# Macaron block on one core: where the output products, the query products, the value tiles and GpSimd's order stand

## The chip, the core and the metric

The kernel runs on one core of a Trainium2 chip. The core has five engines that run their own instruction streams: TensorE (PE; its weight loads are shown as PEld), VectorE (DVE), ScalarE (ACT), GpSimd (POOL) and SyncE (SP), which here only issues transfers. The metric is the device time of one execution in microseconds (us), median of several runs. Lower is better.

## The reference, cut to what matters

All data are float32. A block with half-weighted feed-forward parts on both sides of an attention:

```python
x = x + 0.5 * ffn(layernorm(x))          # x: 4 batches x 256 tokens x 512
x = x + attn(layernorm(x))
x = x + 0.5 * ffn(layernorm(x))

def attn(x):                             # 32 query heads, 8 key/value heads, head size 128
    q, k, v = x @ wq, x @ wk, x @ wv     # wq: 512 x 4096, wk and wv: 512 x 1024
    q, k = rope(q), rope(k)
    scores = einsum('bqhgd,bshd->bhgqs', q by groups of 4 heads, k) * 128 ** -0.5
    allowed = (j <= i) & (j > i - 128)   # causal, a window of 128 keys
    out = einsum('bhgqs,bshd->bqhgd', softmax(where(allowed, scores, min)), v)
    return out @ wo                      # wo: 4096 x 512

def ffn(x):                              # base 512 x 512 with bias, 8 low-rank experts of rank 16
    w = top-2 of softmax(x @ W_router.T), renormalised
    return x @ W_base.T + b_base + 2.0 * sum over experts of w * ((x @ A_e.T) @ B_e.T)
```

## The kernel before, in words

The 1024 tokens are eight tiles of 128. They are worked on in two halves `h` of two batches each. Around the attention stands the feed-forward part (`ffn`), cut into one-letter steps (M, X, T, N: normalise and transpose; A: low-rank products; R: the routing, many small VectorE instructions; B: base product; G, L: the gated part and the sum). The strings in `loose` place the second feed-forward part's steps in the last units of the attention loop.

The attention loop runs over *units* `u`, that is `(h, g, b)`: half, key/value group (8 of them, 4 query heads each), batch of the half. A group's two units have `b` = 0 and 1. In the loop `n` is the number of the *next* group, counted from 1. So `n` is odd in one group and even in the other, and a unit with `b = 0` holds the query products of group `n`. A unit with `b = 1` and even `n` holds the key products of two groups.

Three matrix products are done with seven half-size products in place of eight (a Strassen form), for which sums of blocks are made first:

- `queries`: product `n` of seven, 8 matmul instructions each. `product(1)` is copied by ScalarE (`p1c`), `product(6)` added to it (`u2`), and so on. The four results stand in four PSUM banks of the tag `mm`, one for each batch and pair of heads. `turn(b, j, bank)` calls `rope`: three VectorE instructions (`ra`, L368, and two `rb`, L370) that read the bank, and one GpSimd addition (L374) into `qT`.
- `keys`: the same for two groups of keys, in two banks.
- `outputs`: four entries for one unit, `(4)`, `(1, 6)`, `(2, 3)` and `(7, 5)`, named y4, y(1,6), y(2,3), y(7,5) in this text. y4 is 4 matmul instructions, the others 8 each. Each takes one `mm` bank, and VectorE then adds it to `x` (L624) or `z` (L617). They use sums of `oT` (`oTs`, four GpSimd instructions, L120) and sums of `wo` (`wos`, four GpSimd instructions, L125, in `sum_o_weights`). Product 4 reads the fourth of the `wos` instructions' result, product 6 the third `oTs`, product 7 the first `wos`. The entries are put in the queue `late` at the end of a unit, and run in the next one.

Further parts of a unit: `project_v` (pv, L492: a value tile for a later group), `scores` (sa L509 and sb L524 on TensorE; L515 to L531 on VectorE), `exponentials` (`nm`, L537 and L538 on VectorE; L542 on ScalarE), `normalize` (two GpSimd instructions, L551), `transposes` (t, L560; then a ScalarE copy `p0` and two VectorE products L569), and `values` (oa and ob, L582, and two ScalarE copies into `oT`). `scores` of the next unit stand between the `transposes` and the `values` of this one.

What sets the order: inside `tc.manual_schedule(engines=...)` the named engines issue in program order. Elsewhere the framework's list scheduler orders each engine by its own estimate of times: among the instructions that it holds for ready, the one that stands first in the program goes first, and another one may fill a wait. In the kernel before, GpSimd and ScalarE are in program order from the loop on (L732). TensorE and VectorE are left to the list scheduler, and so is GpSimd in the projections ahead of the loop (L696 to L708). Tiles of one tag are handed out in program order. There are four banks of the tag `mm` and four of the tag `s` (transposes and scores), two buffers each for `ra` and `rb`, and one each for `wq`, `wqs`, `wos` and `probs`. A new `wos` can be written only when the matmuls that read the old one are done.

Of the kernel before, what the change touches and what calls it, by code (L numbers as in the profile page):

```python
# [27 lines left out]
TPH = NT // NHALF  # L28
# [9 lines left out]
def macaron_kernel(  # L38
# [99 lines left out]
    def load_o(h, g):  # L138
        wo_g = sb.tile([P, G, D], F32, tag="wo", name=f"wo_{h}_{g}")
        nc.sync.dma_start(out=wo_g, in_=wo[ts(g, G * HD), :].rearrange("(c p) f -> p c f", p=P))  # L140
        weights["o", h, g] = wo_g

    def sum_o_weights(h, g):

        w = weights["o", h, g]
        new = sb.tile([P, 3, 2, D // 2], F32, tag="wos", bufs=1, name=f"wos_{h}_{g}")
        t1 = w[:, :2, D // 2 :]
        if (h, g) == groups[-1]:
            t1 = sb.tile([P, 3, 2, D // 2], F32, tag="wqs", bufs=1, name=f"wot_{h}_{g}")[:, 0]
        weights["os", h, g] = sums_b(  # L150
            w[:, :2, : D // 2], w[:, :2, D // 2 :], w[:, 2:, : D // 2], w[:, 2:, D // 2 :],
            t1, *(new[:, i] for i in range(3)),
        )
# [222 lines left out]
    def sum_tokens(h):  # L376

        sums = sb.tile([P, 4, 2, S], F32, tag="xs", bufs=1, name=f"xs_{h}")
        (b11, b12), (b21, b22) = ((xa[h][:, c : c + 2, :S], xa[h][:, c : c + 2, S:]) for c in (0, 2))
        t1, t2, t3, t4 = (sums[:, i] for i in range(4))  # L380
        for dst, p, q in ((t1, b12, b11), (t2, b22, t1), (t3, b22, b12), (t4, b21, t2)):
            nc.vector.tensor_tensor(dst, p, q, ALU.subtract)
        xs[h] = (b11, b21, b22, t4, t1, t2, t3)

    def add(dst, bank, other):
        nc.vector.tensor_tensor(dst, bank, other, ALU.add)

    def temp(name, at):
        return sb.tile([HD, TH], F32, tag=name, bufs=1, name=f"{name}_{at}")

    def queries(h, g):


        state = {}

        qT[h, g] = sb.tile([HD, BPH, S // BLK, G, BLK], F32, tag="qT", name=f"qT_{h}_{g}")

        def product(n, bank=None):
            w, x = weights["qs", h, g][n - 1], xs[h][n - 1]
            new = bank is None  # L400
            if new:
                bank = mm_bank(f"q{n}_{h}_{g}")
            for j in range(2):
                for c in range(2):
                    nc.tensor.matmul(  # L405
                        bank[:, ts(j, S)], w[:, c, ts(j, HD)], x[:, c, :],
                        start=(new and j == 0 and c == 0), stop=(c == 1), skip_group_check=True,
                    )
            return bank

        def turn(b, j, src):
            rope(
                qT[h, g][:, b, :, j : j + 2, :], src, f"q_{h}_{g}_{b}_{j}",
                lambda t: t.rearrange("p (j e q) -> p e j q", j=2, q=BLK),
            )

        def first():
            state["p1"] = product(1)
            state["p1c"] = temp("p1c", f"q_{h}_{g}")
            nc.scalar.copy(state["p1c"], state["p1"])  # L420

        def sixth():
            state["p6"], state["u2"] = product(6), temp("u2", f"q_{h}_{g}")
            add(state["u2"], state["p6"], state["p1c"])

        def fifth():
            state["p5"], state["v1"] = product(5), temp("v1", f"q_{h}_{g}")
            add(state["v1"], state["p5"], state["u2"])

        def seventh():
            state["p7"] = product(7)
            add(state["p6"], state["p7"], state["v1"])
            turn(1, 2, state["p6"])

        def second():
            turn(0, 0, product(2, state["p1"]))

        def third():  # L440
            product(3, state["p5"])

        def turn_third():
            add(state["p5"], state["p5"], state["u2"])
            turn(1, 0, state["p5"])

        def fourth():
            bank = product(4, state["p7"])
            add(bank, bank, state["u2"])
            turn(0, 2, bank)  # L450

        return [first, sixth, fifth, seventh, second, third, turn_third, fourth]

    def keys(h, g):

# [119 lines left out]
    def values(h, g, b, p0, p1):  # L575
        oT = sb.tile([HD, G, S], F32, tag="oT", bufs=4, name=f"oT_{h}_{g}_{b}")
        v = vS[h, g - g % 2]
        cols = ts(g % 2, HD)
        for i, parts in enumerate(([p0], p1)):
            po = mm_bank(f"o{'ab'[i]}_{h}_{g}_{b}")  # L580
            for n, part in enumerate(parts):
                nc.tensor.matmul(  # L582
                    po, v[:, 2 * b + n, cols], part, start=(n == 0), stop=(n == len(parts) - 1)
                )
            nc.scalar.copy(  # L585
                oT[:, :, ts(i, P)].rearrange("p j (e q) -> p e j q", e=2),
                po.rearrange("p (e j q) -> p e j q", e=2, j=G),
            )
        return oT
# [71 lines left out]
    def norm_attn(t):  # L661
        h, i = divmod(t, TPH)
        if i == 0:
            xa[h] = sb.tile([P, KC, TH], F32, tag="xa", name=f"xa_{h}")
        norm(t, xa[h], i, "a")
# [23 lines left out]
    for h, order in (  # L689
# [3 lines left out]
        for step in order.split():  # L693
            halves[h](step)
    norm_attn(behind.popleft())
    sum_tokens(0)  # L696
    sum_weights("k", *groups[0])
    sum_weights("q", *groups[0])
    keys(*groups[0])
    load_k(*groups[2])  # L700
    for step in queries(*groups[0]):
        step()
    load_q(*groups[1])
    sum_weights("q", *groups[1])
    for i in range(TPH):
        project_v(0, 0, i)
    load_v(*groups[2])
    load_o(*groups[1])  # L708

    late, slow = deque(), {}

    def run(queue, n):
        for _ in range(min(n, len(queue))):
            queue.popleft()()
# [1 line left out]


    loose = {
        8: ("0M0 0M1 1M0 1M1", "", ""), 5: ("0X0 0X1", "", ""), 4: ("0T0 0T1 0A0 0A1 0R", "", ""),
        3: ("", "0B0 0B1", "0G 1X0 1X1"), 2: ("0L0 0L1 1T0 1T1 1A0 1A1 1R", "", ""),
        1: ("1B0 1B1", "", "1G 1L0 1L1"),
    }

    def fill(left, place):
        for step in loose.get(left, ("", "", ""))[place].split():
            slow[int(step[0])](step[1:])
# [2 lines left out]
    ctx.enter_context(  # L732
        tc.manual_schedule(engines={mybir.EngineType.Pool, mybir.EngineType.Activation})
    )
    ahead = scores(*units[0])
    exponentials(*ahead)
    for u, (h, g, b) in enumerate(units):
        n = groups.index((h, g)) + 1
        left = len(units) - u
        at = n + n % 2  # L740
        if at < len(groups):
            project_v(*groups[at], 2 * (1 - n % 2) + b)
        normalize(ahead[0], ahead[2])
        fill(left, 0)
        if b == 0 and n < len(groups):
            for step in queries(*groups[n]):
                step()
            if n % 2 == 0:
                sum_weights("k", *groups[n])
        elif b == 1 and n % 2 == 0 and n < len(groups):  # L750
            keys(*groups[n])
            if n + 2 < len(groups):
                load_k(*groups[n + 2])
        run(late, len(late))
        if b == 0:
            sum_o_weights(h, g)
            if n + 1 < len(groups):
                load_q(*groups[n + 1])
            if 1 < n < len(groups):
                load_o(*groups[n])  # L760
        else:
            if g == NKV - 2 and h + 1 < NHALF:
                sum_tokens(h + 1)
            if n + 1 < len(groups):
                sum_weights("q", *groups[n + 1])
                if n % 2 == 0 and n + 2 < len(groups):
                    load_v(*groups[n + 2])
        fill(left, 1)
        p0, p1 = transposes(h, g, b, ahead[0])
        fill(left, 2)  # L770
        if left > 1:
            ahead = scores(*units[u + 1])
        oT = values(h, g, b, p0, p1)
        if left > 1:
            exponentials(*ahead)
            if left == 2:
                nc.scalar.activation(root, eps, AF.Sqrt)
            late.extend(outputs(h, g, b, oT))
        if (h, g) == groups[-1]:
            if b == 0:  # L780
                late.append(lambda: add_sums(h, 0))
        elif g == NKV - 1:
            late.append(lambda h=h, b=b: add_sums(h, b))
            slow[b] = ffn(tiles(h, b, 1), "f2", store)
        elif (h, g) == groups[-2] and b == BPH - 1:
            late.append(lambda h=h, b=b: add_sums(h, b))
# [56 lines left out]
```

## Time and profile before

| | |
|---|---|
| time, median of 3 runs | 819.4 us (818.27 to 820.91) |
| the profiled execution's own time | 820.07 us |
| its span | 818.2 us |
| TensorE matmuls busy | 786.0 us, 96% |
| VectorE, GpSimd, ScalarE busy | 517.4, 473.4, 221.2 us |
| mean granted TensorE clock | 0.994 |

The span goes from the first to the last instruction of the profiled execution; 1.9 us of its time lie outside it. The feed-forward part and the projections fill some 94 us. The attention loop runs from there to about 785 us, and the second feed-forward part ends the program. In the middle of the loop a stretch of two groups (four units) takes 85.6 to 86.2 us, again and again. A matmul's end in the profile is modelled, so that the starts of successive matmuls tell more than their durations: 8 matmuls of a query product start 1.73 us before the next product's, though the row says 1.89.

### The profile page before, as it was taken

The numbers are of one execution on the slowest core, as the hardware profiler recorded it, in microseconds if no ns is written. First come the engines' busy times: TensorE is split into PE (matmuls) and PEld (weight loads), VectorE is DVE, ScalarE is ACT, GpSimd is POOL, SyncE is SP. The second block draws the span as 40 slices with busy tenths as digits, with TensorE's granted clock in tenths as the row PEclk, the third lists the DMA queues.
The fourth block names the chain that finished last, engine by engine and source line by source line (L and its number), as shares of the span: only waits on it lengthen the run. The fifth ranks groups of instructions, "written<-read, shape, count | busy, mean of one in ns | idle before, by whom it ended". The sixth has DMA issues, their size and how long they took to land.

```text
span 818.2 us, 10473 instructions
## 1 busy us (share of the span) xinstructions
PE 786.0 (96%) x3620; PEld 622.8 (76%) x3620; DVE 517.4 (63%) x1266; ACT 221.2 (27%) x774; POOL 473.4 (58%) x492
## 2 busy tenths in 40 slices
PE   6999888999999999999999999999999999989998
PEld 4458677888788887887878788888888788766654
DVE  4558572766566665668578937683867566663673
ACT  5242314122312222222222142204023312323332
POOL 6411548575757584767576566757575757663511
PEclk9999899999999999999999999999999999999999
DMA  9300210211113021303030303120201111010001
GB/s 314 124 1 26 78 52 1 103 52 52 52 52 104 14 90 33 122 0 103 1 129 27 103 1 110 45 85 19 103 27 52 52 52 52 1 51 27 1 26 52
DMA packets 29332, 48.92 MB, mean 60 GB/s; under 512 B 1120, under 2 KB 10080, under 8 KB 29280
## 3 DMA queue, kind: packets, MB, share of 16 engines
q1 hardware_dynamic: 29280, 48.26, 17.6%
q8 instruction: 29, 0.48, 0.2%
q14 instruction: 23, 0.19, 0.1%
HBM read 46.15 MB, written 2.10 MB: 59 GB/s over the span
## 4 chain that ended last, share of the span: by engine, by line
PE 74%; DVE 13%; POOL 7%; issue 3%; DMA 1%; ACT 1%; SPq 0%; DVEq 0%; POOLq 0%; ACTq 0%
PE y L608 18%; PE q L405 13%; DVE rb_q L370 8%; PE ob L582 7%; PE k L463 6%; PE pv L492 6%; PE sb L524 5%; PE po_f L335 5%; PE sa L509 3%; PE oa L582 3%; POOL qT L374 3%; DVE ra_q L368 3%; PE t L560 3%; PE po_f L347 2%; PE pa_f L322 1%
## 5 line engine op out<-in xcount | busy, mean ns | idle before, releaser
L374 POOL TENSOR_TENSOR qT<-ra_q,rb_q 128x512 f32<-128x512 f32 x64 | 81.2, 1270 | 147.5 <-DVE rb_q L370 147.5
L608 PE MATMUL y<-wo,oT 128*128 128x256 f32 x368 | 95.7, 382 | 9.1 <-DVE rb_q L370 9.1
L564 ACT COPY p<-t 128x512 f32<-128x512 f32 x32 | 18.8, 587 | 274.9 <-PE t L560 274.9
L370 DVE TENSOR_TENSOR rb_q<-q,sin_sb 64x512 f32<-64x512 f32 x128 | 88.1, 688 | 1.7
L608 PEld LDWEIGHTS y<-wo,oT 128*128 128x128 f32 x368 | 68.6, 190 | 21.0 <-issue 11.0
L551 POOL TENSOR_TENSOR probs<-probs,sm 128x512 f32<-128x512 f32 x64 | 65.2, 1039 | 10.1 <-DVE sm L546 9.1
L120 POOL TENSOR_TENSOR oTs<-oT 128x256 f32<-128x256 f32 x62 | 45.5, 734 | 43.0 <-ACT oT L585 40.6
L608 PE MATMUL y<-wos,oTs 128*128 128x256 f32 x248 | 65.0, 384 | 0.9 <-POOL oTs L120 0.9
L492 PEld LDWEIGHTS pv<-wv,xa 128*128 128x128 f32 x256 | 49.7, 194 | 19.2 <-issue 13.4
L546 DVE RECIPROCAL sm<-sm 128x8 f32<-128x8 f32 x32 | 6.5, 202 | 91.2 <-ACT probs L542 91.2
L582 PE MATMUL ob<-p,v 128*128 128x512 f32 x128 | 60.4, 593 | 2.3 <-DVE p L569 2.3
L492 PE MATMUL pv<-wv,xa 128*128 128x256 f32 x256 | 61.8, 386 | 0.0
L405 PE MATMUL q<-xs,wqs 128*128 128x256 f32 x256 | 60.9, 379 | 0.5 <-DVE rb_k L370 0.5
L405 PE MATMUL q<-xa,wq 128*128 128x256 f32 x256 | 60.6, 379 | 0.0
L405 PE MATMUL q<-xs,wq 128*128 128x256 f32 x256 | 60.5, 379 | 0.0
L335 PE MATMUL po_f<-wb_sb,xn_f 128*128 128x512 f32 x128 | 57.8, 593 | 0.0
L624 DVE TENSOR_TENSOR x<-y,x 128x256 f32<-128x256 f32 (+1 forms) x62 | 34.2, 555 | 33.2 <-PE y L608 32.6
L405 PEld LDWEIGHTS q<-xs,wqs 128*128 128x128 f32 x256 | 48.4, 190 | 7.4 <-DVE rb_k L370 0.9
L405 PEld LDWEIGHTS q<-xs,wq 128*128 128x128 f32 x256 | 48.6, 190 | 6.7
L405 PEld LDWEIGHTS q<-xa,wq 128*128 128x128 f32 x256 | 48.6, 190 | 6.6
L608 PEld LDWEIGHTS y<-wos,oTs 128*128 128x128 f32 x248 | 45.8, 190 | 9.7 <-POOL oTs L120 2.1
L374 POOL TENSOR_TENSOR kT<-ra_k,rb_k 128x512 f32<-128x512 f32 x16 | 20.3, 1271 | 53.6 <-DVE rb_k L370 53.6
(156 smaller groups left out, 1640.1 us busy)
## 6 DMA issues: line engine op xcount, KB each, us to landing
wq<-in_wq_dram SPq DMA_DIRECT2D x16, 1024.0 KB, 5.5
wo<-in_wo_dram SPq DMA_DIRECT2D x16, 1024.0 KB, 5.2
wk<-in_wk_dram SPq DMA_DIRECT2D x8, 512.0 KB, 3.4
wv<-in_wv_dram SPq DMA_DIRECT2D x8, 512.0 KB, 3.4
x<-in_x_dram SPq DMA_DIRECT2D x8, 256.0 KB, 6.5
out_dram<-x SPq DMA_DIRECT2D x8, 256.0 KB, 2.0
wb_sb<-in_w_base_dram SPq DMA_DIRECT2D x1, 1024.0 KB, 6.9
ar_sb<-in_w_ar_dram SPq DMA_DIRECT2D x1, 272.0 KB, 4.1
```

The lines of the kernel that those rows point to most:

```text
L120: nc.gpsimd.tensor_tensor(dst, p, q, op)
L335: nc.tensor.matmul(po[i], x_of(i, c), wb_sb[:, c, :], start=(c == 0), stop=False)
L370: nc.vector.tensor_tensor(twice(b[o : o + half, :]), twice(src[i : i + half, :]), angle(sin_sb[o : o + half, :]), ALU.mult,)
L374: nc.gpsimd.tensor_tensor(dst, view(a), view(b), ALU.add)
L405: nc.tensor.matmul(bank[:, ts(j, S)], w[:, c, ts(j, HD)], x[:, c, :], start=(new and j == 0 and c == 0), stop=(c == 1), skip_group_check=True,
L463: nc.tensor.matmul(dst, w[n - 1][:, c, :], x[n - 1][:, c, :], start=(start and c == 0), stop=(c == 1), skip_group_check=True,)
L492: nc.tensor.matmul(pv[:, : 2 * HD], xa[h][:, c, ts(i, P)], weights["v", h, g][:, c, :], start=(c == 0), stop=(c == KC - 1),)
L524: nc.tensor.matmul(pb[:, ts(e, 3 * BLK)], q[:, 2 + e, 2 * p : 2 * p + 2, :], k[:, n - P : n + BLK], start=True, stop=True,)
L551: nc.gpsimd.tensor_tensor(w, w, sm[:, n : n + G].unsqueeze(2).to_broadcast([P, G, P]), ALU.mult)
L582: nc.tensor.matmul(po, v[:, 2 * b + n, cols], part, start=(n == 0), stop=(n == len(parts) - 1))
L608: nc.tensor.matmul(py[:, ts(i, D // 2)], lhs[n - 1][:, c, :], weights["os", h, g][n - 1][:, c, :], start=(i == 0 and c == 0), stop=(c == 1 ...
L624: nc.vector.tensor_tensor(dst, py[:, : len(which) * D // 2], dst, ALU.add)
```

## The change

- `queries` makes its products in the order 1, 6, 7, 5, 2, 4, 3 in place of 1, 6, 5, 7, 2, 3, 4. `v1` is then made with product 7, and product 5 completes the bank of product 6. The two `turn`s of batch 0 follow products 2 and 4. The two of batch 1 are a last step of their own, `turn_second_batch`.
- GpSimd is in program order from L696 on. In the projections the sums of the next group's `wq` stand ahead of batch 1's `turn`s.
- Of the first group's four value tiles, two are projected ahead of the loop. The other two, and the first of group 2, come in the first unit, between the scores of the next unit and the values. The sums of the first group's `wo` stand ahead of the loop.
- In a unit with `b = 0` that has a next group, y4 alone runs ahead of the transposes. All but the last entry of `late` run behind them (that is y(1,6) and y(2,3)), and the last one behind the next unit's scores (y(7,5); at the start of the second half the last entry is `add_sums`, so that y(7,5) too runs ahead of the scores). The sums of `wo` come after that.
- Of the second feed-forward part, step R of the first batch moves from the start of its unit to behind y4, and a base product moves from behind the outputs to the start of the next unit.

```diff
-        def fifth():
-            state["p5"], state["v1"] = product(5), temp("v1", f"q_{h}_{g}")
-            add(state["v1"], state["p5"], state["u2"])
-        def seventh():
-            state["p7"] = product(7)
-            add(state["p6"], state["p7"], state["v1"])
-            turn(1, 2, state["p6"])
+        def seventh():
+            state["p7"], state["v1"] = product(7), temp("v1", f"q_{h}_{g}")
+            add(state["v1"], state["p7"], state["u2"])
+        def fifth():
+            state["p5"] = product(5)
+            add(state["p6"], state["p5"], state["v1"])
         def second():
             turn(0, 0, product(2, state["p1"]))
-        def third():
-            product(3, state["p5"])
-        def turn_third():
-            add(state["p5"], state["p5"], state["u2"])
-            turn(1, 0, state["p5"])
         def fourth():
             bank = product(4, state["p7"])
             add(bank, bank, state["u2"])
             turn(0, 2, bank)
-        return [first, sixth, fifth, seventh, second, third, turn_third, fourth]
+        def third():
+            product(3, state["p5"])
+            add(state["p5"], state["p5"], state["u2"])
+        def turn_second_batch():
+            turn(1, 2, state["p6"])
+            turn(1, 0, state["p5"])
+        return [first, sixth, seventh, fifth, second, fourth, third, turn_second_batch]
...
+    ctx.enter_context(tc.manual_schedule(engines={mybir.EngineType.Pool}))
     sum_tokens(0)
...
-    for step in queries(*groups[0]):
+    *first_steps, turn_rest = queries(*groups[0])
+    for step in first_steps:
         step()
     load_q(*groups[1])
     sum_weights("q", *groups[1])
-    for i in range(TPH):
+    turn_rest()
+    for i in range(2):
         project_v(0, 0, i)
...
-        8: ("0M0 0M1 1M0 1M1", "", ""), 5: ("0X0 0X1", "", ""), 4: ("0T0 0T1 0A0 0A1 0R", "", ""),
-        3: ("", "0B0 0B1", "0G 1X0 1X1"), 2: ("0L0 0L1 1T0 1T1 1A0 1A1 1R", "", ""),
+        8: ("0M0 0M1 1M0 1M1", "", ""), 5: ("0X0 0X1", "", ""), 4: ("0T0 0T1 0A0 0A1", "0R", ""),
+        3: ("0B0", "0B1", "0G 1X0 1X1"), 2: ("0L0 0L1 1T0 1T1 1A0 1A1 1R", "", ""),
...
+    sum_o_weights(*groups[0])
     ahead = scores(*units[0])
...
-        if at < len(groups):
+        if 0 < u and at < len(groups):
             project_v(*groups[at], 2 * (1 - n % 2) + b)
...
-        run(late, len(late))
+        run(late, 1 if b == 0 and n < len(groups) else len(late))
         if b == 0:
-            sum_o_weights(h, g)
...
         p0, p1 = transposes(h, g, b, ahead[0])
         fill(left, 2)
+        run(late, len(late) - 1)
         if left > 1:
             ahead = scores(*units[u + 1])
+        run(late, len(late))
+        if b == 0 and u > 0:
+            sum_o_weights(h, g)
+        if u == 0:
+            for i in range(2, TPH):
+                project_v(0, 0, i)
+            project_v(*groups[2], 0)
         oT = values(h, g, b, p0, p1)
```

## The prediction

> **What bounds the kernel now.** I read the page first: TensorE is busy 96% of the span at a mean clock of 0.994, so only its gaps can be won. Then I read its timeline. In the middle of the loop the busy time by stage leaves little:
>
> ```profile
> 265.99:351.77 85.78, 84.72 (x406) 70.45 (x405) 55.44 (x130) 20.59 (x83) 55.40 (x55) 1.00 0.19 62
> ```
>
> Four units take 85.78 us and TensorE (second number) works 84.72 of them. What it waits for there stands in its timeline (odd group, `b = 0`, then `b = 1`):
>
> ```profile
> 283.51 1.03 PE L608 MATMUL y<-wos,oT 128*128 128x256 f32 x4
> ...
> 287.16 1.10 PE L608 MATMUL y<-wo,oT 128*128 128x256 f32 x4 [0.57 <-DVE rb_q L370]
> ...
> 297.92 1.03 PE L608 MATMUL y<-wos,oT 128*128 128x256 f32 x4
> ...
> 299.64 1.03 PE L608 MATMUL y<-wos,oTs 128*128 128x256 f32 x4
> ```
>
> The query products end at 283.51; y(2,3) then waits 0.57 for a bank that a rope still reads. Product 4 (297.92) and product 6 (299.64) of the next unit start without a wait. VectorE and GpSimd in the same unit:
>
> ```profile
> 279.34 0.69 DVE L368 TENSOR_TENSOR ra_q<-q,cos_sb 128x512 f32<-128x512 f32 x1
> ...
> 287.75 1.39 DVE L370 TENSOR_TENSOR rb_q<-q,sin_sb 64x512 f32<-64x512 f32 x2
> ...
> 294.86 1.02 DVE L537 TENSOR_SCALAR nm<-mx 128x4 f32<-128x4 f32 x1
> ```
>
> ```profile
> 290.47 1.30 POOL L125 TENSOR_TENSOR wos<-wo 128x512 f32<-128x512 f32 x1
> ...
> 294.58 1.28 POOL L125 TENSOR_TENSOR wos<-wo,wos 128x512 f32<-128x512 f32 x1
> 297.05 0.73 POOL L120 TENSOR_TENSOR oTs<-oT 128x256 f32<-128x256 f32 x1 [1.20 <-ACT oT L585]
> ...
> 298.66 0.73 POOL L120 TENSOR_TENSOR oTs<-oT 128x256 f32<-128x256 f32 x1
> ```
>
> The four ropes and two additions run without a break from 279.34 to 289.14, 9.80 us. The `wos` sums take 290.47 to 295.86; product 6 needs the third `oTs`, done at 299.39, and starts 0.25 later. That is all the slack there is. The first unit is another matter:
>
> ```profile
> 94.77 1.22 PE L509 MATMUL sa<-kT,qT 128*128 128x64 f32 x4 [3.97 <-POOL qT L374]
> ...
> 119.93 1.98 PE L582 MATMUL ob<-p,v 128*128 128x512 f32 x4 [2.32 <-DVE p L569]
> 121.75 1.89 PE L492 MATMUL pv<-wv,xa 128*128 128x256 f32 x8
> 125.88 1.13 PE L608 MATMUL y<-wos,oT 128*128 128x256 f32 x4 [2.24 <-POOL wos L125]
> ```
>
> **First unit, 83 to 133 us.** Lost now: 3.97 for `qT`, whose GpSimd addition (93.45) stands behind three `wqs` sums; after it the granted clock is 0.50 from 94.27 to 101.10 (sb takes 2.77 for 1.47, pv 3.26 for 1.89, sa a little more: about 3.0); then 2.32 (`p`, behind the ropes), 2.24 (`wos`), 0.30 (`oTs`), and some 0.1 at each restart (0.4). Sum 12.2.
>
> After: product 5 still ends at about 79.6 and product 2 is done by 75.3, so batch 0's ropes run from about 80 to 85.4, and their second `qT` is done by 86.7. Products end at 83.0 and two value tiles fill 3.45. The second needs the bank that the rope frees at 85.4: about 0.7 lost. Scores go at 87 with no half clock. SP may issue the next `wq` once product 4 has read the old one, now the sixth product and not the seventh: 1.7 earlier; it lands 5.5 later (page), at about 87. GpSimd then sums it until 92.4, adds batch 1's `qT` (2.5), sums `wo` (5.4, the row above), normalises (2.1): 102.4. TensorE runs products 1, 6, 7, 5 from 89.4 to 96.3. Product 2 reuses the bank that `p1c` must first leave; that copy stands on ScalarE behind the exponentials, and these wait for score work queued behind the ropes on VectorE: about 97.5, 1.2 lost. The products end at 102.8, when `normalize` is just done; transposes, scores and three value tiles (5.2) then cover the ropes that end at 109.7, and `wos` has long been there. Lost after: 1.9. Gain 12.2 - 1.9, say **10.4**; bounds 5 (the tiles don't fill, each wait half returns) and 12.2.
>
> **The b = 0 units of the loop.** All times here in the frame of the rows above. Removed: the wait for the bank (0.57, with restarts and the second start 0.8). Added: batch 0's first rope needs product 2, the fifth, so it starts at 280.06 + 0.20 = 280.26 in place of 279.34, and VectorE ends at 290.06, 0.92 later. Banks come free at 282.4, 285.3, 288.0, 290.1. TensorE: y4 (0.86) and eight transposes (0.87) reach 285.25; y(1,6) waits 0.2 for the second bank and ends at 287.15; y(2,3) waits for 288.15, of which some scores fill about 0.5, as three transposes fill today. So about 0.7 is lost, no less than now: splitting the outputs cancels only against the later ropes.
>
> Then the sums of `wo`. They are four instructions, 5.39 us with their gaps, and the first must wait until product 7 has read the old `wos`. Product 7 now stands behind the scores: 283.51 + 0.86 + 0.87 + 1.73 + 1.73 + 2.20 (scores) + 0.86 = 291.76, plus the lost 0.7, plus 0.2 to reach GpSimd: 292.65 in place of 290.47. Queued behind on GpSimd stand the `oTs` sums and `normalize`. `wos` ends at 298.05; TensorE, with pv done at 297.6, waits about 0.5 for it at product 4. Three `oTs` (2.34) end at 300.4, so product 6 starts at about 300.45: 0.8 later than now. `normalize` ends at 303.3, before the transposes at about 304.8. So an **odd group costs 0.8 more**: five of them 4.0; in group 9 `late` has a fifth entry, y(7,5) precedes the scores, and I count 0.1.
>
> In an **even group** the `wks` sums (3.15) lie between `qT` and `wos`, which cover the wait for product 7. There the 0.92 of VectorE passes on: `qT`, `wks` and `wos` end 0.92 later, where y4 has 0.72 of slack (338.76 to 339.48). Product 4 is a filler among the key products; TensorE waits for it, 0.25 later than today. Seven groups: 1.8. Sum of the loop: 4.0 + 0.1 + 1.8, **+5.9**; bounds -2 (no loss before product 7, GpSimd just in time) and +11 (no filler for y(2,3): 0.5 more in odd groups, and as much in even ones).
>
> [...] The new place puts `wos` under the next scores' `nm`. The row: L537 takes 1.02 at 294.86 while `wos` runs, against 0.16 for L538 behind it; exponentials start at 296.87, behind ScalarE's `oT` copy, 0.9 after `nm`. [...] I take the row: 0.
>
> **The end, 695 to 745 us.** Today step R's instructions run ahead of the ropes: gaps of 1.02 and 1.16 at 716 and 719, then 0.77 and 0.36 in the next unit, which has no value tile; with restarts 4.1. After: ropes start with product 2 and 0.7 is lost; the base product (3.43) stands where a value tile stood and covers the `oT` and `oTs` waits. R then delays only L569. Gain **3.4**; bounds 1.5 and 4.1.
>
> The other edits (order of `load_q`, `load_v`, `load_o` on SP, program order on GpSimd for the early `wks` and `wqs` sums) cost nothing: `wq` loads waited up to 38 us for their buffer and still have most of a group, the early sums end at 29.5, and products start at 62. Without that cover each would cost one load, 5.5.
>
> Sum: -10.4 + 5.9 - 3.4 = -7.9. The profiled execution took 820.07 (span 818.2 and 1.9 around it), 0.67 above the median; against the median 819.4 - 7.9 = **811.5**.
>
> **The rivals.**
> 1. *GpSimd keeps up*: y6 and y4 find their sums and the outputs fill the ropes. For it: GpSimd is busy 58%. Against it: 0.25 us of slack at product 6. The 0.8 of 14 groups goes: -10.4 - 3.4 - 11 gives 794.5. 12%.
> 2. *The first unit yields half*: a new wait for `p1c` or `normalize` in place of the old ones, for GpSimd in program order holds `normalize` behind 13 us of sums. -5.5 + 5.9 - 3 gives 817. 15%.
> [...]
> 4. *It doesn't do what it says*: VectorE and TensorE stay with the list scheduler, which could draw y(7,5) ahead of the scores. Then the loop is even and the first unit remains: 807; inside the forecast's range.
>
> **How the numbers follow.** About 0.3%, 2.5 us, is what a measurement of this kernel can tell from no change. Forecast with case 4: 61%, 806 to 816, all faster. Case 1 faster; of case 2 a third faster, most within; case 3 slower. Faster 0.61 + 0.12 + 0.05 = 0.78, same 0.10, slower 0.12. The range 798 to 819 leaves out case 3 and the lower part of case 1.
>
> **What would show it.** Right: no gap at the first scores, clock 1.00 from 83 on, the first outputs about 10 us earlier; in the loop `rb_q` gaps at y(2,3) remain at about 0.5, `wos` starts after product 7, and y gets gaps from `wos` and `oTs` of 0.5 and 0.7 in odd groups; four units take about 86.8 in place of 85.8. Wrong: four units under 85, a half clock in the first unit, or gaps at `p1c` in even units.

## The result and the profile after

The changed kernel takes 812.6 us (median, 812.4 to 815.0), the kernel before 819.6 beside it on the same chip: a ratio of 0.992, 95% interval 0.990 to 0.995. It is 7.0 us faster.

The profiled execution of the changed kernel is the slowest of its four: span 813.1, its own time 815.0. Its span is 5.1 under that of the kernel before, so the profile shows less gain than the medians do. Both profiled executions, before and after, have 3.4 us at a granted clock of 0.50 in the feed-forward part ahead of the attention, from 32.8 and 32.9 us on. The other three executions of the changed kernel show a mean clock of 1.000 in place of 0.998, so they can't have had it. To keep this out, I count all steps below from the first query product.

First the page's line of busy times, after. TensorE works 786.7 us in a shorter span, as before; only gaps have gone:

```profile
PE 786.7 (97%) x3620; PEld 621.4 (76%) x3620; DVE 516.5 (64%) x1266; ACT 221.6 (27%) x774; POOL 472.3 (58%) x492
```

Busy time by stage (window, its length, then busy PE, PEld, DVE, ACT, POOL, the granted clock, two DMA columns): first the kernel before, in its first unit, then the changed kernel in the same window and in four units of the loop.

```profile
83.00:136.00 53.00, 44.15 (x204) 37.09 (x203) 29.02 (x74) 13.37 (x46) 31.66 (x28) 0.94 0.16 50
```

```profile
83.00:136.00 53.00, 52.24 (x255) 44.05 (x254) 31.82 (x81) 17.76 (x66) 36.05 (x34) 1.00 0.16 50
266.00:353.00 87.00, 85.39 (x405) 70.44 (x404) 54.87 (x130) 20.69 (x83) 55.10 (x55) 1.00 0.19 61
```

The first unit is full now, at a clock of 1.00 in place of 0.94. In the loop four units take 87.1, where they took 85.8, and TensorE stands idle for 1.6 of the 87.0 us in the window.

TensorE's timeline in the first unit, after (start, duration, line, operands; in brackets the idle time ahead and what ended it). The scores (sa) start without a wait where 3.97 stood, `ob` and y4 as well where 2.32 and 2.24 stood; 0.70 for `wqs` is the one new gap:

```profile
86.81 1.05 PE L509 MATMUL sa<-kT,qT 128*128 128x64 f32 x8
...
91.59 3.72 PE L405 MATMUL q<-xs,wqs 128*128 128x256 f32 x16 [0.70 <-POOL wqs L120]
...
111.44 1.88 PE L582 MATMUL ob<-p,v 128*128 128x512 f32 x4
...
114.88 1.03 PE L608 MATMUL y<-wos,oT 128*128 128x256 f32 x4
```

The same view in the loop, after: y4 of an even group's `b = 1` unit (243.95), then an odd group, with y(1,6), y(2,3) and the first half of y(7,5) of its `b = 0` unit, and products 4 and 6 of its `b = 1` unit:

```profile
243.95 1.13 PE L608 MATMUL y<-wos,oT 128*128 128x256 f32 x4 [0.57 <-POOL wos L125]
...
275.86 1.10 PE L608 MATMUL y<-wo,oT 128*128 128x256 f32 x4
...
278.63 1.13 PE L608 MATMUL y<-wo,oT 128*128 128x256 f32 x4 [0.19 <-DVE rb_q L370]
...
281.98 1.03 PE L608 MATMUL y<-wos,oTs 128*128 128x256 f32 x4
...
288.45 1.13 PE L608 MATMUL y<-wos,oT 128*128 128x256 f32 x4 [0.27 <-POOL wos L125]
...
290.74 1.13 PE L608 MATMUL y<-wos,oTs 128*128 128x256 f32 x4 [0.29 <-POOL oTs L120]
```

The wait for the ropes' bank has shrunk from 0.57 to 0.19, and waits for GpSimd's sums have come in its place. GpSimd and VectorE in the same unit:

```profile
283.09 1.27 POOL L125 TENSOR_TENSOR wos<-wo 128x512 f32<-128x512 f32 x1 [1.04 <-PE y L608]
...
287.13 1.26 POOL L125 TENSOR_TENSOR wos<-wo,wos 128x512 f32<-128x512 f32 x1
...
289.96 0.72 POOL L120 TENSOR_TENSOR oTs<-oT 128x256 f32<-128x256 f32 x1
```

```profile
279.31 1.39 DVE L370 TENSOR_TENSOR rb_q<-q,sin_sb 64x512 f32<-64x512 f32 x2
...
285.83 1.25 DVE L537 TENSOR_SCALAR nm<-mx 128x4 f32<-128x4 f32 x1
```

Product 7 (281.98) is the last reader of the old `wos`. The first sum starts right after it, at 283.09, after an idle 1.04 that the view puts down to y. The ropes end at 280.70, which is 6.83 after the query products' end at 273.87; before, it was 5.63.

The end, after: y(1,6) still waits 0.95 in the last unit with ropes. The base product, 3.4 long, runs at 725.22 and covers what y waited for there:

```profile
714.80 1.10 PE L608 MATMUL y<-wo,oT 128*128 128x256 f32 x4 [0.95 <-DVE rb_q L370]
...
725.22 3.60 PE L335 MATMUL po_f<-wb_sb,xn_f 128*128 128x512 f32 x8
```

All versions can be compared step by step, since one stage repeats to 0.01 us from group to group. The table gives the change of each step against the kernel before, in us, from the starts of each unit's first `ob` product in the profiled executions. A step ends at the `ob` of the unit that it is named for. "First" goes from the first query product to the second unit. Typical groups are shown once, and single ones differ from them by up to 0.4; "n = 7" and "n = 9" are both units of that group; "last" is the last unit with ropes, "base" the next one; "end" is the sum of all steps.

```
                                 first   odd n       even n      n=7    n=9   last   base   end
                                         b=0   b=1   b=0   b=1
changed kernel                   -11.8  -0.26 +1.11 -0.34 +0.83 +2.00  -0.03  -1.01  -1.63   -5.2
old order and outputs in loop    -12.0   0.00  0.00  0.00  0.00 -0.06   0.00  +0.08  -1.63  -13.6
old order in loop                -11.8  -0.73 +1.10 -0.73 +0.11 +1.44  -0.33  -0.70  -1.63  -15.5
old outputs                      -12.0  -0.03  0.00 -0.10 +0.61 +1.49  +1.81  -0.69  -1.63   -7.3
y(7,5) first                     -11.9  -0.02  0.00 -0.10 +0.62 +1.50  +1.05  -1.02  -1.63   -8.1
y(7,5) first, old order          -12.0  -0.33  0.00 -0.33  0.00 -0.23  -0.33  -0.23  -1.63  -18.2
two wos, early sums              -11.8  -0.26  0.00 -0.33  0.00 +0.39  -0.03  +1.74  -1.63  -14.4
two wos, early sums, old order   -11.9  -0.73  0.00 -0.73  0.00 -1.02  -0.32  -0.63  -1.63  -22.5
```

So the changed kernel gains 11.8 in the first unit and 2.6 at the end, and gives back 9.2 in the loop: -5.2. The medians hold 1.8 more. The half clock ahead of the first query product can be most of it: 3.4 us at half speed are 1.7 us, and three of the changed kernel's four runs went without. But the kernel before runs with different mean clocks too (0.991 to 0.996 beside the experiments), so how much of these 1.8 us the change has earned is open.

### The profile page after: what moved, and what is told of

Read it like the earlier page. It is cut to its first block, busy times and chain, and to the rows that moved or that the text cites. A ratio compares the mean times of both kernels' runs of the same rounds, so it can differ in the third digit from the quotient of the medians.

```text
span 813.1 us, 10427 instructions
## 1 busy us (share of the span) xinstructions
PE 786.7 (97%) x3620; PEld 621.4 (76%) x3620; DVE 516.5 (64%) x1266; ACT 221.6 (27%) x774; POOL 472.3 (58%) x492
## 4 chain that ended last, share of the span: by engine, by line
PE 62%; POOL 16%; DVE 15%; issue 3%; DMA 2%; ACT 1%; SPq 0%; DVEq 0%; POOLq 0%; ACTq 0%
PE y L608 15%; PE q L405 15%; DVE rb_q L370 8%; POOL wos L125 6%; PE po_f L335 5%; PE k L463 4%; PE ob L582 4%; PE sb L524 4%; PE pv L492 4%; DVE ra_q L368 3%; DVE q L386 2%; POOL wks L120 2%; PE sa L509 2%; PE oa L582 2%; POOL wo L125 2%
## 5 line engine op out<-in xcount | busy, mean ns | idle before, releaser
L608 PE MATMUL y<-wo,oT 128*128 128x256 f32 x368 | 97.1, 386 | 4.7 <-DVE rb_q L370 4.3
L608 PEld LDWEIGHTS y<-wo,oT 128*128 128x128 f32 x368 | 67.5, 190 | 17.1 <-DVE rb_q L370 4.2
L608 PE MATMUL y<-wos,oTs 128*128 128x256 f32 x248 | 64.3, 382 | 2.3 <-POOL oTs L120 2.3
L546 DVE RECIPROCAL sm<-sm 128x8 f32<-128x8 f32 x32 | 6.5, 202 | 92.0 <-ACT probs L542 91.8
L492 PE MATMUL pv<-wv,xa 128*128 128x256 f32 x256 | 60.1, 379 | 0.0
L405 PE MATMUL q<-xs,wqs 128*128 128x256 f32 x256 | 58.5, 379 | 0.7 <-POOL wqs L120 0.7
L585 ACT COPY oT<-oa 128x512 f32<-128x512 f32 x32 | 18.7, 585 | 145.5 <-PE oa L582 145.5
L624 DVE TENSOR_TENSOR x<-y,x 128x256 f32<-128x256 f32 (+1 forms) x62 | 34.4, 554 | 32.8 <-PE y L608 32.2
L368 DVE TENSOR_TENSOR ra_q<-q,cos_sb 128x512 f32<-128x512 f32 x64 | 44.2, 691 | 16.9 <-PE q L405 14.9
L608 PEld LDWEIGHTS y<-wos,oTs 128*128 128x128 f32 x248 | 46.2, 190 | 10.0 <-POOL oTs L120 4.3
```

Source lines behind the costliest of these rows:

```text
L368: nc.vector.tensor_tensor(twice(a), twice(src), angle(cos_sb), ALU.mult)
L405: nc.tensor.matmul(bank[:, ts(j, S)], w[:, c, ts(j, HD)], x[:, c, :], start=(new and j == 0 and c == 0), stop=(c == 1), skip_group_check=True,
L492: nc.tensor.matmul(pv[:, : 2 * HD], xa[h][:, c, ts(i, P)], weights["v", h, g][:, c, :], start=(c == 0), stop=(c == KC - 1),)
L608: nc.tensor.matmul(py[:, ts(i, D // 2)], lhs[n - 1][:, c, :], weights["os", h, g][n - 1][:, c, :], start=(i == 0 and c == 0), stop=(c == 1 ...
L624: nc.vector.tensor_tensor(dst, py[:, : len(which) * D // 2], dst, ALU.add)
```

## The experiments

Eleven versions of the changed kernel, each run four to six times, with the kernel before beside it. They ran in groups on three chips, where the kernel before took 817.7 to 818.6, so the ratios and the table compare better than the times. In those with the old query order, line numbers behind L451 are 18 higher: L626 there is the output product L608, and L600 is `ob`.

**Which edits cost the loop its 9.2?** Query order and place of the outputs, each as it was, singly and together.

```diff
 queries():  # old query order, for all groups but the first
+        if (h, g) != groups[0]:
+            return [first, sixth, fifth_old, seventh_old, second, third_old, turn_third, fourth]
 loop:       # old outputs
-        run(late, 1 if b == 0 and n < len(groups) else len(late))
+        run(late, len(late))
         if b == 0:
+            if u > 0:
+                sum_o_weights(h, g)
...
-        run(late, len(late) - 1)
...
-        run(late, len(late))
-        if b == 0 and u > 0:
-            sum_o_weights(h, g)
```

Both undone:

> The changed kernel with the loop's query order and the place of its outputs and `wo` sums as before; the first unit and the end keep the change. Theory: the first unit earns 11.7 and the end 2.6, and the loop gives 9.2 back only through these two edits, so without them the time is 819.6 - 14.3 = about 805, four units take 85.8 again. Rival: the loop's loss comes from what is left here (program order on GpSimd, the new orders of loads), then it stays near 812 and four units near 87.

Measured: 804.9 us, ratio 0.984 (0.983 to 0.986). Every step of the loop is back to 0.00. The loss comes from these two edits and from nothing else; GpSimd's program order and the orders of loads cost the loop nothing.

The query order alone undone:

> The changed kernel, but with batch 1's query products where they were (ropes start after the third product); outputs stay on both sides of the transposes. Theory: batch 0 first makes all of VectorE's work of a group 0.9 to 1.2 us later, and that is the larger part of the loop's loss. Undone, y(2,3) no longer waits (0.7 less in each group), an even group's `wos` is there in time, an odd group still waits about 0.8 at product 6 for the `wo` sums behind product 7: loop -4 to -2 against the kernel before, 801 to 803. Rival: the loss comes from product 7 standing behind the scores (the outputs); then this version still loses in the loop and takes 810 to 812.

Measured: 803.0 us, ratio 0.982 (0.981 to 0.984), with every sign as the theory has it. TensorE's timeline in an odd group:

```profile
272.71 1.10 PE L626 MATMUL y<-wo,oT 128*128 128x256 f32 x4
...
283.16 1.13 PE L626 MATMUL y<-wos,oT 128*128 128x256 f32 x4 [0.27 <-POOL wos L125]
...
285.45 1.13 PE L626 MATMUL y<-wos,oTs 128*128 128x256 f32 x4 [0.29 <-POOL oTs L120]
```

The outputs behind the transposes now find every bank free: 0.73 gained in a typical `b = 0` unit. The loop now gains 1.4 in place of losing 9.2. The waits of 0.27 and 0.29 at products 4 and 6 are those of the changed kernel to the hundredth, so the odd groups' 1.1 has nothing to do with the query order. The even groups' 0.83 has: it falls to 0.11.

The outputs alone undone:

> The changed kernel, but with all outputs ahead of the transposes and the `wo` sums behind them, as before; query products stay with batch 0 first. Theory: the ropes end 0.9 to 1.2 later and y(2,3) takes all of it as a wait of some 1.5 us at its bank in each of 12 groups, so the loop loses 10 to 12 and the time is 815 to 817, slower than the changed kernel. Rival (the outputs alone cause the loop's loss): 805, and y<-wos and y<-oTs without a gap.

Measured: 811.8 us, ratio 0.993 (0.992 to 0.994). The forecast of 815 to 817 failed, and so did its reason. TensorE's timeline in a `b = 0` unit, after the even group's y4:

```profile
243.21 1.13 PE L608 MATMUL y<-wos,oT 128*128 128x256 f32 x4 [0.33 <-POOL wos L125]
...
275.12 1.10 PE L608 MATMUL y<-wo,oT 128*128 128x256 f32 x4 [0.42 <-DVE rb_q L370]
...
277.25 0.78 PE L509 MATMUL sa<-kT,qT 128*128 128x64 f32 x6
277.88 1.13 PE L608 MATMUL y<-wo,oT 128*128 128x256 f32 x4
...
279.71 0.38 PE L509 MATMUL sa<-kT,qT 128*128 128x128 f32 x2
```

Later ropes should have made y(2,3) wait 1.5. It starts at 277.88 without a wait; only y(1,6), at 275.12, waits 0.42. With batch 0 first, that batch's `qT` is ready while batch 1's ropes still run, and its scores (sa) fill the time between the outputs. The `b = 0` units lose nothing. What remains is the even group's wait for `wos`, 0.6 with its restart, and single groups (n = 7, n = 9).

**Is it product 7 behind the scores?** One line puts y(7,5) ahead of them:

```diff
         fill(left, 2)
-        run(late, len(late) - 1)
+        run(late, len(late))
```

> The changed kernel with y(7,5) ahead of the scores instead of behind them, nothing else. Theory: product 7, the last reader of the old `wos`, then ends 2.2 us earlier, GpSimd starts the `wo` sums that much earlier, and the 1.1 us that each odd group loses at products 4 and 6 goes to nothing (5 groups, and 1.2 of group n=7). An even group's 0.83 falls only to about 0.7, since it comes from the later ropes. The loop then loses 2 to 3 in place of 9: 805 to 807. Rival: the odd groups' loss comes from the later ropes as well (GpSimd late at `qT`); then nothing changes, 812, or the scores that come 0.9 later make it 814.

Measured: 810.2 us, ratio 0.990 (0.989 to 0.992). The mechanism holds in the odd groups. GpSimd's and TensorE's timelines in an odd group:

```profile
279.31 1.27 POOL L125 TENSOR_TENSOR wos<-wo 128x512 f32<-128x512 f32 x1
```

```profile
285.53 1.03 PE L608 MATMUL y<-wos,oT 128*128 128x256 f32 x4
...
287.26 1.03 PE L608 MATMUL y<-wos,oTs 128*128 128x256 f32 x4
```

The sums follow `qT` without a gap and products 4 and 6 wait for nothing: +1.11 becomes 0.00 in the odd groups. The sum was 4 us off (the loop loses 6.4, not 2 to 3): y(7,5) behind the scores had also given the last rope 0.25 more time in each `b = 0` unit, and that is lost (-0.26 becomes -0.02). Group n = 9 loses 1.05 where I had counted nothing.

With the old query order as well:

> Both undone: y(7,5) ahead of the scores, and in the loop batch 1's query products first; of the split outputs there remains that the transposes stand between y4 and y(1,6). Theory, by adding what the runs before showed: each b = 0 unit gains 0.73 (y(2,3) finds its bank), odd groups lose nothing, even groups nothing; loop -9 to -10, first unit -12, end -2.3: 794 to 797, the fastest so far. Rival: with y(7,5) ahead of the scores the outputs again meet the ropes, and the 0.73 falls to the 0.33 that group n=9 shows in the version with the old order: 799 to 801.

Measured: 800.2 us, ratio 0.979 (0.977 to 0.981). Here the rival was right: 0.33 in each `b = 0` unit, not 0.73. Of all groups only n = 7 still waits for a sum (0.35, for `oTs`).

**Take away the wait itself.** With a second `wos` buffer (its room is taken from `xc` and `oTs`, one buffer less each) the sums needn't wait for product 7, and they can run where GpSimd stands idle ahead of the first `qT` (6.76 in the changed kernel).

```diff
-        new = sb.tile([P, 3, 2, D // 2], F32, tag="wos", bufs=1, name=f"wos_{h}_{g}")
+        new = sb.tile([P, 3, 2, D // 2], F32, tag="wos", bufs=2, name=f"wos_{h}_{g}")
...
+        if b == 0 and u > 0:
+            sum_o_weights(h, g)
         if b == 0 and n < len(groups):
             for step in queries(*groups[n]):
...
-        if b == 0 and u > 0:
-            sum_o_weights(h, g)
```

> The changed kernel with two `wos` buffers (room from `xc`, 3 to 2, and `oTs`, 2 to 1) and the `wo` sums ahead of the query additions on GpSimd, where it stands idle for 5.7 to 6.8 us in each b = 0 unit; the sums need 5.4. So no `wo` sum waits for product 7 or for the ropes. Theory: product 4's 5.9 us and product 6's 2.3 of waits in the loop go, and with them most of the loss; what remains is y(2,3) behind the ropes (3.1). 812.6 - 8 to -9 = 804; 801 if TensorE's restarts and the bank waits shrink as well. Rival: VectorE is what sets the pace (ropes later, `oT` and exponentials later); then TensorE waits at score work or p1c for what it no longer waits for here, and the time stays over 809.

Measured: 805.6 us, ratio 0.985 (0.984 to 0.986). All `b = 1` units but that of n = 7 are at 0.00, so the 0.83 and the 1.11 were both the lateness of the `wo` sums and of what stands behind them on GpSimd. But the last unit with ropes lost 1.74 in place of gaining 1.01. VectorE, GpSimd and TensorE there:

```profile
693.66 0.68 DVE L386 TENSOR_TENSOR u_q<-q,p1c_q 128x512 f32<-128x512 f32 x1
694.26 0.15 DVE L273 TENSOR_REDUCE r_f<-k_f 128x2 f32<-128x16 f32 x1
...
697.93 1.11 DVE L281 TENSOR_TENSOR s_f<-k_f,r_f 128x16 f32<-128x16 f32 x1
```

```profile
697.74 1.27 POOL L125 TENSOR_TENSOR wos<-wo,wos 128x512 f32<-128x512 f32 x1
```

```profile
700.67 1.97 PE L405 MATMUL q<-xa,wqs 128*128 128x256 f32 x8 [1.68 <-DVE q L386]
```

A step of R of 16 elements a row (L281) takes 1.11 and ends at 699.04, just after the `wos` sum at 699.01. The addition of a query product stands behind it and four more such steps on VectorE, and TensorE waits 1.68 for its bank.

So the last version leaves these sums late in that one group, and takes the old query order:

```diff
-        if b == 0 and u > 0:
+        if b == 0 and u > 0 and n != len(groups) - 1:
             sum_o_weights(h, g)
...
+        if b == 0 and n == len(groups) - 1:
+            sum_o_weights(h, g)
```

> The version with two `wos` buffers and early `wo` sums, now with batch 1's query products first in the loop, and with the sums in the last group that has queries at their late place (there they ran under the small VectorE steps of R, each of which then took up to 1.1 us in place of 0.17). Theory: nothing is left to wait for: b = 0 units gain 0.73, b = 1 units lose nothing, the last groups lose nothing: 794 to 797. Rival: VectorE's operations under GpSimd's early sums get longer (as those of R did) and the query additions come later: 800 or more.

Measured: 797.6 us, ratio 0.974 (0.972 to 0.976): the fastest of all, if 0.6 above what was expected. Busy time by stage over four units:

```profile
259.00:344.00 85.00, 84.98 (x409) 70.97 (x408) 53.23 (x129) 21.27 (x89) 55.91 (x56) 1.00 0.19 62
```

By this view TensorE is idle for 0.02 of 85.00. What is left to win in these groups is TensorE's own work.

**What earned the first unit?** From the version with the loop as before (804.9), one further edit undone at a time.

Without GpSimd's program order in the projections:

```diff
-    ctx.enter_context(tc.manual_schedule(engines={mybir.EngineType.Pool}))
     sum_tokens(0)
```

> The first of these versions (loop's query order and outputs as before), now without GpSimd's program order from the projections on: the list scheduler places GpSimd's work in the first unit again. Theory: in the first unit the program order puts `qT` ahead of nothing and behind the `wqs` sums as the scheduler did, and what earned the 11.8 is above all batch 0 first and the two value tiles; so at most 3 of the 11.8 are lost: 805 to 808. Rival: GpSimd's order alone earns the first unit (a `qT` addition behind three sums, `wos` late, half clock): 812 to 816.

Measured: 809.9 us, ratio 0.990 (0.988 to 0.992). In the first unit 0.9 is lost: a `qT` addition slips between the `wqs` sums again, and the next product waits 1.68 for them in place of 0.5. The larger loss is one that I had not looked for. TensorE and GpSimd in the feed-forward part:

```profile
34.09 0.47 PE L341 MATMUL ph_f<-ident,hl_f 128*128 128x128 f32 x1 [4.27 <-POOL hl_f L290]
```

```profile
32.42 1.26 POOL L125 TENSOR_TENSOR wos<-wo 128x512 f32<-128x512 f32 x1
33.64 1.48 POOL L290 TENSOR_TENSOR hl_f<-hl_f,pe_f 128x128 f32<-128x128 f32 x4
```

The list scheduler pulls three of the `wo` sums that the change put ahead of the loop to 29.7 to 33.7, ahead of the gating `hl_f`. TensorE waits 4.27 there, where the kernels before and after wait 1.45 and 1.51, and the granted clock is 0.50 from 32.4 to 39.1. So the program order is needed because of the other edit.

Batch 1's query products first in the first group too:

```diff
-        if (h, g) != groups[0]:
+        if True:
             return [first, sixth, fifth_old, seventh_old, second, third_old, turn_third, fourth]
...
-    *first_steps, turn_rest = queries(*groups[0])
-    for step in first_steps:
+    for step in queries(*groups[0]):
         step()
...
-    turn_rest()
```

> The first of these versions, with batch 1's query products first in the first group as well; GpSimd adds all four `qT` ahead of the `wqs` sums, the value tiles stay in the first unit. Theory: batch 0 first is what earns most of the first unit: without it batch 0's `qT` is the last of four, done at about 91, while TensorE has products until 83 and two value tiles until 86.5; 4 to 5 us idle, a half clock after it as in the kernel before, and the `wqs` sums 2.5 later: 6 to 10 of the 11.8 are lost, 811 to 815. Rival: GpSimd's order (no `qT` behind `wqs` sums) earns it; then at most 3 are lost, 805 to 808.

Measured: 812.7 us, ratio 0.993 (0.991 to 0.995); by its steps 5.6 of the 12.0 are lost. (The medians lie 7.7 apart; the profiled execution is the fastest of its six.) TensorE's timeline:

```profile
87.49 1.97 PE L405 MATMUL q<-xa,wq 128*128 128x256 f32 x8 [0.79 <-DMA wq<-in_wq_dram]
90.46 0.71 PE L527 MATMUL sa<-kT,qT 128*128 128x64 f32 x4 [1.01 <-POOL qT L374]
...
94.37 3.39 PE L405 MATMUL q<-xs,wqs 128*128 128x256 f32 x8 [2.54 <-POOL wqs L120]
```

The first product of the next group waits for its `wq`, which now lands later, the scores of batch 0 wait for `qT`, and the `wqs` sums behind four `qT` cost 2.54 more; the granted clock is 0.50 from 93.83 to 97.24. This version undoes two things at once, the order of the products and the `wqs` sums' place ahead of batch 1's `qT`, and the 5.6 is for both.

The value tiles where they were:

```diff
-    for i in range(2):
+    for i in range(TPH):
         project_v(0, 0, i)
...
-        if 0 < u and at < len(groups):
+        if at < len(groups):
...
-        if u == 0:
-            for i in range(2, TPH):
-                project_v(0, 0, i)
-            project_v(*groups[2], 0)
```

> The first of these versions, with the value tiles where they were (four ahead of the loop, group 2's at the start of the first unit). Theory: the products then end at 83 and four tiles cover the ropes as well, but none is left behind the first unit's scores, where three tiles (5.2 us) cover the second group's ropes and `p`: the kernel before lost 2.32 there and 2.24 for `wos`; of these `wos` stays early. 2 to 4 are lost: 807 to 809. Rival: the tiles' place is worth nothing, since the other edits have taken the waits that they cover: 805.

Measured: 807.7 us, ratio 0.987 (0.985 to 0.989); 3.2 by the steps. TensorE's timeline, and busy time by stage with the clock:

```profile
111.39 3.02 PE L600 MATMUL ob<-p,v 128*128 128x512 f32 x4 [2.31 <-DVE p L587]
```

```profile
112.20:115.60 3.40, 3.40 (x7) 1.80 (x6) 1.71 (x12) 1.15 (x5) 0.49 (x1) 0.50 0.00 0
```

The wait for `p` of the kernel before (2.32) is back, and after it 3.4 us at half clock: the four `ob` take 3.02 for 1.88.

The end's edit undone:

```diff
-        4: ("0T0 0T1 0A0 0A1", "0R", ""), 3: ("0B0", "0B1", "0G 1X0 1X1"),
+        4: ("0T0 0T1 0A0 0A1 0R", "", ""), 3: ("", "0B0 0B1", "0G 1X0 1X1"),
```

> The first of these versions with the last units' routing and base product where they were. Theory: this edit alone earns what that version gains at the end (0.0 in unit 28 and -1.63 in unit 29), so 1.6 is lost: 806.5. Rival: R ahead of the ropes costs again what the kernel before shows at its two waits of 1.0 and 1.2 in unit 28, 2 more: 808 to 809.

Measured: 806.3 us, ratio 0.986 (0.983 to 0.988). The base step goes from -1.63 to -0.01, all else is as it was. TensorE's timeline, y4 and product 6 where the base product had stood:

```profile
715.56 1.10 PE L626 MATMUL y<-wos,oT 128*128 128x256 f32 x4 [0.77 <-ACT oT L603]
...
717.88 1.13 PE L626 MATMUL y<-wos,oTs 128*128 128x256 f32 x4 [0.35 <-POOL oTs L120]
```

So the base product earns the 1.6, and R's place nothing in this version. The 1.0 that the changed kernel gains in the unit before it comes from its query order and its outputs: that step is +0.08 with both as before, -0.70 and -0.69 with one of them as before, and -1.01 with both changed. R's place was not undone alone in the changed kernel.

## Why the prediction was right, point by point

The time (811.5 against 812.6) and the three signs held. That the time came so close is in part luck. By the steps the change is -5.2 where the three terms sum to -7.9, and the medians hold 1.8 more, which no term of the forecast stands for. Two of the three terms were off by more than the time was.

- **First unit, forecast -10.4, measured -11.8.** The chain held: no gap at the first scores, clock 1.00, `wos` long done. Of the 1.9 said to remain, the bank wait and the `p1c` wait did not come; 0.70 for `wqs` did. (12.2 less 1.9 is 10.3; the 10.4 is a slip.) Undone one at a time, batch 0 first with the earlier `wqs` sums is worth 5.6, the tiles 3.2, GpSimd's order 0.9. That leaves 2.3 of 12.0; the early `wo` sums, which took away the wait of 2.24, were not undone alone.
- **Odd groups, forecast +0.8, measured +0.85** (-0.26 and +1.11). Product 7, first `wos` sum, product 4, product 6: each row stands within 0.1 of where it was put (the frames lie 9.64 apart). The 1.11 is 0.56 of waits for `wos` and `oTs` and some 0.27 more at each of the two restarts. In n = 9, where y(7,5) precedes the scores, the `b = 1` unit is at 0.00, and moving y(7,5) took the 1.11 away in every other odd group but n = 7.
- **Even groups, forecast +0.25, measured +0.50** (-0.34 and +0.83). This is the step that failed, by a mis-sized term: how much later the ropes end. In these groups it is 1.13 and not 0.92 (6.68 us after the query products, before 5.55). The forecast was read from an odd group; here the old first rope stands 0.08 earlier, and ropes and additions take 9.93, not 9.80. The rest is the restart of TensorE. Product 7 has no part in it: with y(7,5) early, an even group's two steps also sum to +0.5 (-0.10 and +0.62), and with the old query order to -0.6. In an even group, y4 behind the query products (TensorE) and the last rope (VectorE), before and then after:

```profile
323.42 1.03 PE L608 MATMUL y<-wos,oT 128*128 128x256 f32 x4
327.58 1.39 DVE L370 TENSOR_TENSOR rb_q<-q,sin_sb 64x512 f32<-64x512 f32 x2
```

```profile
314.62 1.03 PE L608 MATMUL y<-wos,oT 128*128 128x256 f32 x4
319.91 1.39 DVE L370 TENSOR_TENSOR rb_q<-q,sin_sb 64x512 f32<-64x512 f32 x2
```

- **Group n = 7**, counted at 0.8 as one of five odd groups, loses 2.0. The next half's token sums (L382) fall into its ropes and its `wo` sums, and TensorE waits longer for `wos` and `oTs` there, below; no run tried these sums alone.

```profile
376.48 1.13 PE L608 MATMUL y<-wos,oT 128*128 128x256 f32 x4 [0.76 <-POOL wos L125]
...
379.54 1.13 PE L608 MATMUL y<-wos,oTs 128*128 128x256 f32 x4 [1.07 <-POOL oTs L120]
```

- **The loop in all: forecast +5.9, measured +9.2**, inside the bounds. Of the 3.3 between them, the even groups have 2.1 and n = 7 has 1.2. "No less than now" for y(2,3) does not fit the forecast's own rows: product 7 at 291.76 + 0.7 puts the next `ob` 0.3 earlier than in the kernel before, and 0.26 to 0.34 is what a typical group gains there.
- **The end, forecast -3.4, measured -2.6.** The base product covers what it should (1.63). In the unit before, 0.7 of loss was to remain, but y(1,6) and y(2,3) wait 0.95 and 0.19 for the ropes' banks there, with two restarts.
- **`nm` under the `wo` sums, forecast 0.** L537 takes 1.25 there, after the 1.02 of the row before, and TensorE waits nowhere for `nm`: 0 was right. But GpSimd and VectorE held each other up on the path twice: in n = 7 (L382 1.75 in place of 0.68, L125 1.74 in place of 1.27), and in the version with early sums under R (L281 1.11 in place of 0.17), there with 2.7 us. The instructions held there (L382, L281) are of the kind `tensor_tensor`.
- **Case 3, slower, with a chance of 0.12.** No run shows the loss that stands for it: the change takes 812.6 and its versions 797.6 to 812.7, all below the kernel before. What the loop lost in the changed kernel, 9.2, shows as waits for banks, `wos` and `oTs` with their restarts, none of it for `nm`.
- **Rival 1** (794.5) describes not this change but the version with two `wos` buffers and the old order: 797.6. Its 0.8 a group was there to be won, with a buffer and the old order.
- **Rival 4's** order, y(7,5) ahead of the scores, was put at 807; built as the version y(7,5) first, it takes 810.2.

## What to carry to other kernels

When a step moves behind other work, look for the buffer that its reads hold: here one output product behind the scores held `wos`, and with it eight GpSimd instructions and two products of the next unit. An order that is right once, where nothing covers the start, may be wrong in the loop, where other work does: batch 0 first earned up to 5.6 us in the first unit and cost 10.6 in the loop (+9.2 against -1.4 without it). Count steps from a mark that repeats; then single edits can be read to 0.01 us, far below what the times of whole runs can tell.

## What the runs showed of the hardware

In the version with early sums, steps of R from tile to tile that take two tiles were held when they started under a running GpSimd instruction (L281: 1.11 in place of 0.17). Six of them (L269, L272, L274, L278, L279, L281) ended each 0.03 us after the GpSimd instruction that they had started under. `nm` was held in the same way in the changed kernel (L537: 1.25 in place of 0.16). Reductions (L273: 0.15), reciprocals (L546: 0.20) and those that read a product's bank (L386: 0.68) were not held. In the profiles before and after, each of 32 `nm` instructions that started 0.2 us or more inside a GpSimd instruction, and as far from its end, ended after it, and none of 39 such reciprocals (L546) did. Two long ones seem to have taken turns in group n = 7. VectorE, then GpSimd there, after:

```profile
374.62 0.68 DVE L382 TENSOR_TENSOR xs<-xa,xs 128x512 f32<-128x512 f32 x1
375.23 1.75 DVE L382 TENSOR_TENSOR xs<-xa 128x512 f32<-128x512 f32 x1
```

```profile
374.69 1.74 POOL L125 TENSOR_TENSOR wos<-wo,wos 128x512 f32<-128x512 f32 x1
376.39 1.17 POOL L120 TENSOR_TENSOR oTs<-oT 128x256 f32<-128x256 f32 x1
```

Alone they take 0.68, 1.27 and 0.73. Their ends alternate: VectorE 375.30, GpSimd 376.43, VectorE 376.98, GpSimd 377.56. From one end to the next is 1.13, 0.55 and 0.58, a little less than each takes alone. So 1.75 and 1.74 look like one waiting for the other and not like both at half speed.

The half clock did not need a gap as long as the 3.97 of the kernel before. With a gap of 2.31 (value tiles where they were) and one of 2.54 (batch 1 first in the first group) came 3.4 us of it, and in the feed-forward part after a wait of 1.45 (before) and one of 1.51 (after). Yet the 2.32 and 2.24 of the kernel before, at 119.93 and 125.88, brought none: its clock is 1.00 from 119.93 to 130.00. Nor do the two waits of 1.68 show any: the eight matmuls behind them take 1.97 (early sums) and 1.99 (without GpSimd's program order), where eight at half clock take 3.39. The share of busy time does not settle it either: in the 3.41 us ahead of the three half clocks of the kernels before and after TensorE was busy for 0, 53 and 55%, but the 3.41 us ahead of the end of the 2.32 have 32%, and the clock stayed full. What decides between these is open.
